# Weighting the quantile sums one step later in a four-layer graph kernel on Trainium2

## The chip, the core and the metric

The kernel runs on one core of one Trainium2 chip. The core has a matrix engine (TensorE, PE in the profile; its weight loads are shown apart as PEld), a vector engine (VectorE, DVE), a scalar engine (ScalarE, ACT), a general one (GpSimd, POOL) and one that here issues all transfers (SyncE, SP). TensorE writes its results to PSUM; VectorE and ScalarE read them there. The metric is device time in microseconds, as the median of several runs; lower is better.

## The reference, cut to what matters

There are 16 graphs of 1024 nodes with 64 channels, each with its own adjacency matrix, and four layers in turn. Every layer normalizes its input, applies a ReLU and adds its result to `x`. Layer 0 is where the change lies: it takes, for every node and channel, a weighted sum of three interpolated quantiles over the node's neighbours (the graph is thinned first), adds it to the node's own value and runs a two-layer perceptron.

```python
TAUS = [0.25, 0.5, 0.75]
QWEIGHTS = [0.25, 0.5, 0.25]
...
for tau, wt in zip(TAUS, QWEIGHTS):
    pos = jnp.clip(tau * (mf - 1.0), 0.0)
    lo = jnp.floor(pos).astype(jnp.int32)
    hi = jnp.ceil(pos).astype(jnp.int32)
    frac = (pos - lo.astype(x.dtype))[..., None]
    q = gather(lo) * (1.0 - frac) + gather(hi) * frac
    agg = agg + wt * q
...
adj_d = _dilate_adj(adj, mask)
agg = _weighted_nanquantile_agg(x, adj_d > 0)
out = (1.0 + EPS_GIN) * x + agg
h = jax.nn.relu(jnp.einsum('bnc,ch->bnh', out, W1) + b1)
y = jnp.einsum('bnh,ho->bno', h, W2) + b2
```

Layer 1 is a mean over neighbours, layer 2 attention with eight heads biased by the adjacency, layer 3 a graph convolution.

## The kernel before

**Two programs woven into one.** `picks` (L771) does layer 0's quantiles and `layers` (L1231) does the rest of every graph. Both are generators. The kernel's last loop draws a piece of `picks`, which gives back a price (0.42 for a step), and then pieces of `layers` until as much is spent; a block of 128 rows of attention for two heads costs 1.0. While the first graph is being picked, there is no layer work yet; after the last graph is picked, `layers` runs alone.

The framework traces the whole program in this way and then orders each engine's instructions at build time. What is traced earlier has the higher priority, but an instruction whose inputs or buffers are not there in the framework's own estimate is passed by others. `tc.issue_after(i)` adds that the instructions traced under it on the engine of `i` stay behind `i`. `adjoining` (L400) uses it to keep a series of matmuls together. On the chip each engine then runs its list in the given order.

**The steps of the picking.** `steps` (L777) lists graph `b` (16), channel group `g` of 8 channels (8), half `t` of 512 nodes (2) and quantile end `q` (6: lower and upper of three quantiles), 1536 in all. Six steps of the same `b`, `g`, `t` are called a group here; there are 256. A turn `n` of the main loop (L894) does, in this order:

- `next(coming)`: a piece of the tables for the next group. In the first two steps of a group the second such call of the turn also makes pair weights `e` (L697, L700) and `cw` (L702).
- `compare(n)` (L805): VectorE forms the mask `le` (L811) and the two masked words `wa` (L813) and `wb` (L815), each of 128x2048 half-precision numbers; TensorE sums them into `prep` and `val` (L826, L831); ScalarE copies these out as `wi` and `vs` (L837 to L840).
- `bits(n-1)` (L843): VectorE takes `bit` out of `wi`, TensorE builds `pz` from `bit` (L851) and `wi` (L852).
- `next(coming)` again.
- `value(n-2)` (L855): VectorE picks `vs` where `pz` tells it to (L859). When `q` is the last of six, TensorE sums the six into `agg` (L865, twelve instructions). VectorE multiplies `agg` by the interpolation coefficients `coef` into `w` (L874), TensorE sums `w` over the quantiles into the eight rows of `acc` (L876), ScalarE copies them back over the first eight rows of `w` (L877), and SP stores these in `z` (L878).
- after the last group of a graph, `leave` (L1036) runs the perceptron on `z`; then `next(behind)`, a piece of the ranking and thinning of the next graph, and the step ends.

**Buffers.** Tiles of one tag share its buffers. Tag a2 has four in SBUF, for `wi`, `bit`, `e`, `w` and a few rarer tiles. Tag pb has two in PSUM, for `agg` and `acc` and for nearly everything that TensorE makes in `layers`: the transposes `pcols` (L451), `ao` (L1183), `pp` (L1194), the projections `pk`, `pq` (L1131) and `pv` (L1143). Tag a4 has four, for `le`, `wa` and `wb`. A tile's buffer is free when its last reader is done; for `w` this is the store at L878.

Of the kernel before, what the change touches and what calls it, by code (L numbers as in the profile page):

```python
# [16 lines left out]
OP = mybir.AluOpType  # L17
# [21 lines left out]
def tile_preln_adj_stack(  # L39
# [30 lines left out]
    nc = tc.nc  # L70
    B, N, D = x.shape
# [12 lines left out]
    def a4(name, shape=(P, N), dt=F32):  # L84
        return sb.tile(list(shape), dt, tag="a4", bufs=4, name=name)
# [11 lines left out]
    def a2(name, shape=(P, 512), dt=F32):  # L97
        return sb.tile(list(shape), dt, tag="a2", bufs=4, name=name)

    def pa(name, shape=(P, 512), dt=F32):  # L100
        return ps.tile(list(shape), dt, tag="pa", bufs=2, name=name)
# [10 lines left out]
    def pb(name, shape=(P, 512), dt=F32):  # L112
        if alone and name != "pcols":
            return pa(name, shape, dt)
        return ps.tile(list(shape), dt, tag="pb", bufs=2, name=name)
# [124 lines left out]
    sel_c = const.tile([P, 8], F32, name="sel_c")  # L240
# [451 lines left out]
    def pair_weights(c0, rk):  # L692


        sh = [P, C, NBK, 2]
        e = a2("e", sh, HP)
        nc.vector.tensor_tensor(  # L697
            e, bc(k16[:, None, :, :], sh), bc(rk[:, :, None, c0 : c0 + 2], sh), OP.subtract
        )
        nc.vector.tensor_scalar(e, e, 0.0, 16.0, op0=OP.max, op1=OP.min)  # L700
        w = sb.tile(sh, I16, tag="cw", bufs=6, name="cw")
        act(w, e, AF.Copy, scale=1024.0)  # L702
        return w.bitcast(HP).rearrange("p c b s -> p c (b s)")
# [67 lines left out]
    def picks():  # L771

        steps = [  # L777
            (b, g, t, q) for b in range(B) for g in range(NG) for t in range(NH) for q in range(NQ)
        ]
        weights, tables, state, vs_of, els = {}, {}, {}, {}, {}  # L780

        def make(el, g, t):
            gen = group(el, g, t, weights)
            tables[el.b, g, t] = next(gen)
            if t == 0 and g < NG - 1:
                todo = [(el, g + 1, 0), (el, g + 1, 1)]
            elif t == 0:
                todo = []
            elif g < NG - 1:
                todo = [(el, g + 1, 2), (el, g + 1, 3)]  # L790
            else:
                todo = [(el.b + 1, 0, pp) for pp in range(4)] if el.b + 1 < B else []
            n = 0
            for _ in gen:
                if n % 2 == 1 and todo:
                    o, g2, pp = todo.pop(0)
                    o = els[o] if isinstance(o, int) else o
                    prepare(o, g2, pp)
                n += 1
                yield None  # L800

        def prepare(el, g, pp):
            weights.setdefault((el.b, g), {})[pp] = pair_weights(8 * g + 2 * pp, el.rk)

        def compare(n):  # L805
            b, g, t, q = steps[n]
            el = els[b]
            hs = slice(t * 512, (t + 1) * 512)
            cum, c1, c0 = tables[b, g, t]
            le = a4("le", (P, 4, 512), HP)  # L810
            nc.vector.tensor_tensor(le, cum, bc(el.krow[q][:, None, hs], [P, 4, 512]), OP.is_lt)  # L811
            wa = a4("wa", (P, 4, 512), HP)
            nc.vector.tensor_tensor(wa, le, c0, OP.mult)  # L813
            wb = a4("wb", (P, 4, 512), HP)
            nc.vector.tensor_tensor(wb, le, c1, OP.mult)  # L815
            prep, val = pa("prep"), pa("val")

            rounds = [
                (prep, [sel_w[:, 1, :]] * 4, [wb[:, pp, :] for pp in range(4)]),
                (prep, [sel_w[:, 0, :]] * 4, [wa[:, pp, :] for pp in range(4)]),  # L820
            ] + [
                (val, [el.tab[:, i, 4 * g + pp, :] for pp in range(4)], [le[:, pp, :] for pp in range(4)])
                for i in range(2)
            ]
            def made():
                yield nc.tensor.matmul(  # L826
                    prep, sel_q[:, q, :], el.kq[:, hs], start=True, stop=False, skip_group_check=True
                )
                for i, (dst, w, r) in enumerate(rounds):
                    for pp in range(4):  # L830
                        yield nc.tensor.matmul(  # L831
                            dst[32 * pp : 32 * pp + 32, :], w[pp], r[pp], start=i == 2, stop=i in (1, 3),
                            tile_position=(0, 32 * pp), skip_group_check=True,
                        )

            adjoining(made())
            wi = a2("wi")  # L837
            act(wi, prep, AF.Identity, bias=shifts[:, 5:6])
            vs = sb.tile([P, 512], F32, tag="v", bufs=8, name="vs")
            act(vs, val, AF.Copy, scale=1.0 / UP)  # L840
            state[n] = [wi, vs]

        def bits(n):  # L843
            wi, vs = state[n]
            bit = a2("bit", dt=I32)
            nc.vector.tensor_scalar(
                bit, wi.bitcast(I32), to30, 0x40000000, op0=OP.logical_shift_left, op1=OP.bitwise_and
            )
            pz = pa("pz")
            up = lambda x: x.bitcast(BF).rearrange("p (n two) -> p n two", two=2)[:, :, 1]  # L850
            nc.tensor.matmul(pz, nth, up(bit), start=True, stop=False)  # L851
            nc.tensor.matmul(pz, plus_k, up(wi), start=False, stop=True)  # L852
            state[n] = [pz, vs]

        def value(n):  # L855
            b, g, t, q = steps[n]
            el = els[b]
            pz, vs = state.pop(n)
            nc.vector.scalar_tensor_tensor(vs, pz, 97.0, vs, op0=OP.is_equal, op1=OP.mult)  # L859
            vs_of[q] = vs  # L860
            if q < NQ - 1:
                return
            agg = pb("agg")
            adjoining(
                nc.tensor.matmul(  # L865
                    agg[32 * (q_ % 4) : 32 * (q_ % 4) + 32, :], sel_t[:, q_ // 4, :], vs_of[q_],
                    start=q_ < 4, stop=q_ > 1, tile_position=(0, 32 * (q_ % 4)),
                    skip_group_check=True,
                )
                for q_ in range(NQ)  # L870
            )
            hs = slice(t * 512, (t + 1) * 512)
            w = a2("w")
            nc.vector.tensor_tensor(w, agg, el.coef[:, hs], OP.mult)  # L874
            acc = pb("acc", (8, 512))
            nc.tensor.matmul(acc, sel_c, w, start=True, stop=True)  # L876
            nc.scalar.copy(w[:8, :], acc)  # L877
            nc.sync.dma_start(el.z[t * D + 8 * g : t * D + 8 * g + 8, t, :], w[:8, :])  # L878

        els[0] = arrive(0)  # L880
        for r in background(0):
            yield 0.0
        for _ in els[0].stages:
            pass
        for pp in range(4):
            prepare(els[0], 0, pp)
        for _ in make(els[0], 0, 0):
            yield 0.05
        coming = behind = stages = iter(())


        STEPS = {12: 1, 11: 2, 10: 2, 9: 2, 8: 2, 7: 5, 6: 4, 5: 1, 4: 1, 3: 1, 2: 1, 1: 2}
        last, per = len(steps), NG * NH * NQ
        for n in range(last + 2):  # L894
            b, g, t, q = steps[min(n, last - 1)]
            to_go = per - n % per
            if n < last:
                if q == 0 and n + NQ < last:
                    coming = make(els[steps[n + NQ][0]], *steps[n + NQ][1:3])
                if to_go == per and b + 1 < B:  # L900
                    behind = background(b + 1)
                next(coming, None)
                compare(n)
                if to_go == 2 * NQ and b + 1 < B:


                    for _ in behind:
                        pass
                    els[b + 1] = arrive(b + 1)
                    stages = els[b + 1].stages  # L910
                for _ in range(STEPS.get(to_go, 0)):
                    next(stages, None)
            if 0 <= n - 1 < last:
                bits(n - 1)
            next(coming, None)
            if 0 <= n - 2:
                value(n - 2)
                if (n - 1) % per == 0:
                    leave(els.pop(steps[n - 2][0]))
                    for _ in stages:  # L920
                        pass
            next(behind, None)
            yield .42
# [356 lines left out]
```

## Time and profile before

| | us |
|---|---|
| median of 3 runs | 13374.41 (13370.68 to 13393.19) |
| the profiled execution's own time | 13383.01 |
| its span, first to last instruction | 13381.0 |
| granted TensorE clock, mean | 0.985 |
| `w` L874, 256 times: busy, idle of VectorE just before | 176.1, 132.5 |
| `agg` L865: PE busy | 592.5 |
| `acc` L876: PE busy | 263.1 |
| copy L877: ScalarE busy, idle just before | 144.9, 131.4 |

The profile is one execution. "Busy" is the time in which an instruction of the group ran; the idle time is that of the same engine directly ahead of such an instruction, with the instruction whose end released it. TensorE's matmuls are pipelined and their ends are modelled, so that its busy share is not a share of its peak. The idle time of one engine matters only where that engine, or one that waits for it, sets the pace.

### The profile page before, as it was taken

What the parts mean: (1) busy time and instruction counts of PE and PEld (TensorE: products, weight loads), DVE (VectorE), ACT (ScalarE), POOL (GpSimd) and SP (SyncE); (2) the same over time, 40 slices, a digit from 0 to 9 for tenths busy, and PEclk for the clock granted to TensorE, in tenths of its full rate; (3) what the DMA queues carried; (4) which work ended last, traced back from release to release, by engine and by line L of the source; (5) the groups of instructions that cost most, each with busy time, mean ns of one, the idle gap of its engine ahead of it and who ended that gap; (6) DMA issues with size and microseconds to landing.
All of it is one profiled execution on the core that took longest, in us unless ns stands there. A gap on an engine that the chain in (4) does not pass through costs nothing. (4 is left out here: it accounts for less than half of the span.)

```text
span 13381.0 us, 221273 instructions
## 1 busy us (share of the span) xinstructions
PE 12224.7 (91%) x86209; PEld 5569.6 (42%) x86209; DVE 11686.7 (87%) x21644; ACT 9477.1 (71%) x16250; POOL 25.6 (0%) x138
## 2 busy tenths in 40 slices
PE   1789999999999999999999999999999999999998
PEld 0224444444444444444444444444444444444445
DVE  8898989899898988989889898998989899887873
ACT  1557777677777776777767777777777777777766
POOL 0000000000000000000000000000000000000000
PEclk9999999999999999999999999999999999999999
DMA  3012121221212112121221212112121121301112
GB/s 100 30 39 66 51 86 49 62 73 53 82 52 88 50 57 75 50 88 52 65 66 56 82 53 70 63 56 81 53 83 48 60 80 52 94 30 60 33 50 74
DMA packets 503196, 841.35 MB, mean 63 GB/s; under 512 B 238720, under 2 KB 273664, under 8 KB 502144
## 3 DMA queue, kind: packets, MB, share of 16 engines
q1 hardware_dynamic: 502144, 827.20, 19.7%
q8 instruction: 675, 11.06, 0.3%
q14 instruction: 377, 3.09, 0.1%
HBM read 616.27 MB, written 206.57 MB: 61 GB/s over the span
## 5 line engine op out<-in xcount | busy, mean ns | idle before, releaser
L727 PE MATMUL px<-valid,cw 128*128 128x512 fp8e4 x8192 | 2072.7, 382 | 0.0
L813 DVE TENSOR_TENSOR wa<-le,c 128x2048 f16<-128x2048 f16 x1536 | 1870.2, 1218 | 152.4 <-PE prep L831 131.5
L811 DVE TENSOR_TENSOR le<-cum,krow 128x2048 f16<-128x2048 int16 x1536 | 1867.8, 1216 | 24.5 <-PE val L831 22.5
L815 DVE TENSOR_TENSOR wb<-le,c 128x2048 f16<-128x2048 f16 x1536 | 1868.8, 1217 | 15.5 <-PE prep L831 15.3
L398 ACT ACTIVATE c<-px,shifts 128x512 f16<-128x512 f32 x2048 | 1414.5, 694 | 347.1 <-PE px L748 172.5
L398 ACT ACTIVATE wi<-prep,shifts 128x512 f32<-128x512 f32 x1536 | 1061.8, 691 | 456.2 <-PE prep L831 364.1
L398 ACT ACTIVATE high<-px,shifts 128x512 f16<-128x512 f32 x1024 | 711.1, 694 | 910.5 <-PE px L727 908.0
L398 ACT ACTIVATE s<-s,nm 128x1024 f32<-128x1024 f32 x1024 | 1167.7, 1143 | 225.2 <-DVE nm L1173 217.4
L1183 PE MATMUL ao<-eT,v 128*64 128x128 f32 x16384 | 1272.4, 278 | 26.5 <-ACT eT L454 23.1
L727 PEld LDWEIGHTS <-cw 128*128 128x128 f16 x8192 | 800.4, 98 | 1147.0 <-issue 322.4
L831 PE MATMUL val<-le,tab 128*32 128x512 f16 x12288 | 1238.7, 386 | 30.1 <-DVE vs L859 22.8
L451 PE MATMUL pcols<-identf,s 128*128 128x128 f32 x8192 | 1175.3, 282 | 84.1 <-ACT eT L454 42.1
L1164 PE MATMUL sp<-kT,qT 64*128 64x512 f32 x4096 | 1166.3, 644 | 61.0 <-DVE nm L1173 59.6
L859 DVE SCALAR_TENSOR_TENSOR vs<-pz,vs 128x512 f32<-128x512 f32 x1536 | 1049.4, 683 | 142.6 <-PE pz L852 135.9
L451 PEld LDWEIGHTS pcols<-identf,s 128*128 128x128 f32 x8192 | 891.5, 141 | 631.0 <-ACT eT L454 252.8
L454 ACT COPY eT<-pcols 128x512 f32<-128x512 f32 x2048 | 1116.4, 597 | 51.9 <-PE pcols L451 47.7
L1183 PEld LDWEIGHTS ao<-eT,v 128*64 128x64 f32 x16384 | 962.6, 136 | 432.8 <-issue 208.9
L398 ACT ACTIVATE vs<-val 128x512 f32<-128x512 f32 x1536 | 923.8, 601 | 259.6 <-PE val L831 156.0
L831 PE MATMUL prep<-wb,sel_w 128*32 128x512 f16 x6144 | 783.1, 392 | 140.8 <-DVE wb L815 133.1
L831 PE MATMUL prep<-wa,sel_w 128*32 128x512 f16 x6144 | 852.4, 384 | 0.0
L1173 DVE CUSTOM_DVE_ANT_0 s<-sp,ad,nm 128x512 f32<-128x512 f32 x1024 | 730.7, 745 | 95.9 <-PE sp L1164 94.8
L1173 DVE CUSTOM_DVE_ANT_0 s<-sp,ad 128x512 f32<-128x512 f32 x1024 | 680.6, 684 | 105.4 <-PE sp L1164 80.1
(263 smaller groups left out, 19193.4 us busy)
## 6 DMA issues: line engine op xcount, KB each, us to landing
ad<-in_adj_dram SPq DMA_DIRECT2D x768, 512.0 KB
adjT_d<-aT SPq DMA_DIRECT2D x128, 512.0 KB
aT<-adjT_d SPq DMA_DIRECT2D x128, 512.0 KB
md<-sm SPq DMA_DIRECT2D x216, 256.0 KB
sb<-md SPq DMA_DIRECT2D x216, 256.0 KB
rem_d<-rem SPq DMA_DIRECT2D x128, 256.0 KB
left_d<-nb SPq DMA_DIRECT2D x128, 256.0 KB
lr<-left_d SPq DMA_DIRECT2D x256, 128.0 KB
```

The source lines that it names most:

```text
L398: nc.scalar.activation(out_, in_, func, **kw)
L451: nc.tensor.transpose(pt[:, c, :], ad[:, (4 * s + c) * P : (4 * s + c + 1) * P], identf)
L454: nc.scalar.copy(aT[:, 4 * s : 4 * s + 4, :], pt)
L727: yield nc.tensor.matmul(px[pp], w[:, j, :], valid[:, j, :], start=False, stop=j == C - 1, skip_group_check=True,)
L811: nc.vector.tensor_tensor(le, cum, bc(el.krow[q][:, None, hs], [P, 4, 512]), OP.is_lt)
L813: nc.vector.tensor_tensor(wa, le, c0, OP.mult)
L815: nc.vector.tensor_tensor(wb, le, c1, OP.mult)
L831: yield nc.tensor.matmul(dst[32 * pp : 32 * pp + 32, :], w[pp], r[pp], start=i == 2, stop=i in (1, 3), tile_position=(0, 32 * pp), skip_gr ...
L859: nc.vector.scalar_tensor_tensor(vs, pz, 97.0, vs, op0=OP.is_equal, op1=OP.mult)
L1164: nc.tensor.matmul(sps[e], qT[e * D : (e + 1) * D, i * P : (i + 1) * P], kT[e * D : (e + 1) * D, hs], start=True, stop=True,)
L1173: nc.vector.tensor_tensor_reduce(ss[e][:, hs], sps[e], ad[:, hs], -1.0, 3.0e38 if t == 0 else nms[e], op0=OP.add, op1=OP.min, accum_out=nm,)
L1183: nc.tensor.matmul(ao[e * D : (e + 1) * D, :], v[:, j, e * D : (e + 1) * D], eTs[e][:, j, :], start=j == 0, stop=j == C - 1, tile_position ...
```

## The change

The last part of `value`, from the multiply of `agg` to the store, becomes a function `weigh` that is put on a list `owing` and called later: in `compare` of the next turn, right after `wb`, with `tc.issue_after` on `wb`. After the last group of a graph it is called at once, before `leave`, with no such order. The multiply, the matmul, the copy and the store are the same; the tiles `w` and `acc` are asked for at the new place, and `agg`, whose matmuls stay where they were, is read there.

```diff
@@ -812,7 +812,9 @@
             wb = a4("wb", (P, 4, 512), HP)
-            nc.vector.tensor_tensor(wb, le, c1, OP.mult)
+            last = nc.vector.tensor_tensor(wb, le, c1, OP.mult)
+            while owing:
+                owing.pop()(last)
             prep, val = pa("prep"), pa("val")
@@ -869,13 +871,17 @@
-            hs = slice(t * 512, (t + 1) * 512)
-            w = a2("w")
-            nc.vector.tensor_tensor(w, agg, el.coef[:, hs], OP.mult)
-            acc = pb("acc", (8, 512))
-            nc.tensor.matmul(acc, sel_c, w, start=True, stop=True)
-            nc.scalar.copy(w[:8, :], acc)
-            nc.sync.dma_start(el.z[t * D + 8 * g : t * D + 8 * g + 8, t, :], w[:8, :])
+            def weigh(behind):
+                hs = slice(t * 512, (t + 1) * 512)
+                w = a2("w")
+                with tc.issue_after(behind.ins) if behind else ExitStack():
+                    nc.vector.tensor_tensor(w, agg, el.coef[:, hs], OP.mult)
+                acc = pb("acc", (8, 512))
+                nc.tensor.matmul(acc, sel_c, w, start=True, stop=True)
+                nc.scalar.copy(w[:8, :], acc)
+                nc.sync.dma_start(el.z[t * D + 8 * g : t * D + 8 * g + 8, t, :], w[:8, :])
+
+            owing.append(weigh)
@@ -916,6 +922,8 @@
                 if (n - 1) % per == 0:
+                    while owing:
+                        owing.pop()(None)
                     leave(els.pop(steps[n - 2][0]))
```

More of the change, by code (lines that the diff above doesn't have):

```diff
@@ L779, in picks @@
         ]
-        weights, tables, state, vs_of, els = {}, {}, {}, {}, {}
+        weights, tables, state, vs_of, els, owing = {}, {}, {}, {}, {}, []
         def make(el, g, t):
```

## The prediction

> **What bounds the kernel now.** I read the page's first part, then busy time by stage, then the groups of VectorE in the first stage, then its waits in the second, and last the order of time around one moved instruction. The page:
>
> ```profile
> span 13381.0 us, 221273 instructions
> ...
> PE 12224.7 (91%) x86209; PEld 5569.6 (42%) x86209; DVE 11686.7 (87%) x21644; ACT 9477.1 (71%) x16250; POOL 25.6 (0%) x138
> ...
> L813 DVE TENSOR_TENSOR wa<-le,c 128x2048 f16<-128x2048 f16 x1536 | 1870.2, 1218 | 152.4 <-PE prep L831 131.5
> ```
>
> TensorE and VectorE are both nearly full, and even the word `wa` waits for TensorE (131.5 us). The table of stages (from:to, length, then busy us of PE, PEld, DVE, ACT, POOL) parts the span where the first graph's picks start, where they end, and where the last graph's picks end:
>
> ```profile
> 370.00:1030.00 660.00, 543.30 (x2973) 164.59 (x2973) 611.25 (x845) 374.05 (x601) 0.00 (x0) 0.95 0.11 35
> 1030.00:12991.00 11961.00, 11280.37 (x80380) 5148.95 (x80378) 10622.33 (x19460) 8804.49 (x15125) 23.07 (x120) 0.99 0.20 63
> 12991.00:13381.00 390.00, 337.80 (x2561) 229.54 (x2560) 148.10 (x475) 231.25 (x421) 1.06 (x7) 0.87 0.26 83
> ```
>
> The first stage, where no layer of a graph runs yet, belongs to VectorE: 611.25 of 660 us, 93%, against 82% for PE. In the long middle stage PE has 94% and VectorE 89%. The tail has none of the moved work but its first instruction. Groups of VectorE in the first stage (busy us, mean ns | idle before, and what ended it):
>
> ```profile
> L811 DVE TENSOR_TENSOR le<-cum,krow 128x2048 f16<-128x2048 int16 x96 | 116.8, 1217 | 0.0
> L813 DVE TENSOR_TENSOR wa<-le,c 128x2048 f16<-128x2048 f16 x96 | 116.8, 1216 | 4.4 <-PE prep L831 4.3
> L815 DVE TENSOR_TENSOR wb<-le,c 128x2048 f16<-128x2048 f16 x96 | 116.8, 1216 | 2.6 <-PE prep L831 2.6
> ...
> L874 DVE TENSOR_TENSOR w<-agg,coef 128x512 f32<-128x512 f32 x16 | 11.1, 691 | 33.1 <-PE pz L851 31.5 <-PE agg L865 1.6
> ```
>
> Of 48.8 us that VectorE idles there, 33.1 lie ahead of the 16 weightings `w`, 2.1 us each. What ends them is `pz` L851, which is not what `w` reads. One of them in order of time (start, us, engine, line):
>
> ```profile
> 574.35 0.59 PE L865 MATMUL agg<-vs,sel_t 128*32 128x512 f32 x1
> ...
> 578.23 0.48 DVE L846 TENSOR_SCALAR bit<-wi,to 128x512 int32<-128x512 int32 x1
> ...
> 578.63 0.69 DVE L697 TENSOR_TENSOR e<-k,rk 128x1024 f16<-128x1024 f16 x1
> ...
> 579.39 0.68 ACT L398 ACTIVATE wi<-prep,shifts 128x512 f32<-128x512 f32 x1
> ...
> 580.91 0.39 PE L851 MATMUL pz<-bit,nth 128*128 128x512 bf16 x1
> ...
> 581.34 0.69 DVE L874 TENSOR_TENSOR w<-agg,coef 128x512 f32<-128x512 f32 x1 [2.02 <-PE pz L851]
> ```
>
> The sum `agg` is finished at 574.9; `w` starts 6.4 us later, right behind the matmul that reads `bit`. So it waits for a buffer: `wi`, `bit`, `e` and `w` share the four of tag a2, and the next `bit`, `e` and `wi` have just taken theirs. Middle stage, who waited for whom (us, times, longest):
>
> ```profile
> DVE xr L1196 <- PE pp L1194: 383.1, 188, 7.3
> DVE vs L859 <- PE pz L852: 131.8, 145, 5.7
> ...
> DVE w L874 <- PE agg L865: 64.0, 75, 5.6
> ...
> DVE w L874 <- PE pz L851: 23.8, 22, 3.9
> ```
>
> Here `w` has 87.8 us, in 97 waits, among far larger ones for PE.
>
> **What the Trainium skill says.** "PSUM — Partial Sum Buffer", section Engine vs sequencer instructions: VectorE's queue is strict first in, first out. The trace agrees: with `w` held 2.02 us nothing else of VectorE starts. "Perfetto Trace Analysis", section Optimization Strategy: the same gap recurring on the engine that should be saturated "can mean there isn't enough SBUF/PSUM for the next tile to be allocated". The gap of about 2 us in 13 of the first 16 groups, ended by a matmul that frees a buffer, is that case.
>
> **The change part by part.** No instruction is added or dropped: each group keeps one multiply (691 ns), two PE passes (592 ns each), one 8-row copy (566 ns mean) and one 16 KB store. For the last group of each graph all is done at once as before, so 240 of 256 groups move.
>
> *Where w goes.* I went through all groups in the trace, against the third `wb` after the last quantile's own (the next step's: a value is formed two steps after its words, in the turn before that `wb`): in 97 of 255 groups `w` starts before that `wb` ends, on average 4.0 us before; in 158 it is already behind it by 6.7 us on average, since there `agg` itself starts 11.6 us after its last input, held off by the two PSUM buffers of tag pb. The new order binds in the 97 only. Idle time before `w`: 63.8 us in the 97, 59.5 in the 158.
>
> *First stage.* 33.1 us of that idle time is here. At the new place, behind `le`, `wa`, `wb` (3 x 1.217 = 3.65 us, more than the usual wait), `pz` has read `bit` and `wi`, so two a2 buffers are free. In the sample `wb` could end near 582.1, where it now ends at 584.6, and `w` would start without a wait, `pz` having ended at 581.3. I leave out the last group (0.4 us, not moved) and 4 to 5 us for waits that come back as `wa` on `prep` or `bit` on a buffer. VectorE sets this stage and the layers can only start behind it: **-28 us**. Bounds: 0, if the wait moves on whole; -33.
>
> *Middle stage, groups that move.* 63.8 - 33.1 = 30.7 us. PE is the fuller engine; an earlier `wa` and `wb` let the next matmuls start earlier, but only where PE would have idled. I take half: **-15 us**. Bounds 0 and -31. The 59.5 us of the other groups I cost at nothing: they wait for `agg`, which doesn't move.
>
> *The agg buffer in PSUM.* It is held until `w` has read it, now a mean of 5.5 us (first matmul to end of `w`, 1413 us in all). The 97 groups hold it 4.0 us longer; in the first stage no layer wants it, leaving 82 x 4.0 = 330 us. From the start of the old `w` to the end of that `wb` (plus 0.7 us), two other tiles of the tag were live for 16.5 of 457 us, and none for 410: these are the very moments when the layers are not using it. All 16.5 us lost would be the most, I take **+12**. If that cover is gone, see the slower rival.
>
> *acc, copy and store.* They follow `w`. `acc` now asks for its buffer behind the layers' requests traced in between. PE's weight load for `acc` waited 63.2 us for `w` already and still will. The copy is ScalarE's, 71% busy. What sits behind the copy on ScalarE is the next `wi`; 0.57 us there is the same work in another place. SP's queue: the store is moved past at most a step's loads and stores (8.3 us: 11961/1440). SP stood 1100.8 us at this store for the copy in the middle stage, but 3762.1 at the adjacency loads for a free buffer, so these loads are not paced by the store. `z` is read only at the end of a graph. GpSimd's queue has none of it. No landing is recorded for the store, so the time that `w` holds its own a2 buffer isn't shown: I take no cost, bounds 0 to +20 (if `bit` waits a quarter of a microsecond in 80 groups).
>
> *Sum:* -28 - 15 + 12 = -31 on the span of 13381.0, 13350. The medians of the runs lie 6.6 us below that span, so the forecast is 13374.4 - 31 = **13343 us**.
>
> **The rivals.** *A, the forecast:* 13315 to 13360.
>
> *B, no measurable change, 13370.* The shortage of a2 buffers only changes hands: `w` keeps a buffer through copy and store while two `wi` and a `bit` want theirs, and `bit` stalls instead; PE absorbs the rest. For it: all four buffers stay, and the majority of groups don't move. Against: in the first two steps of each group only, `e` takes a fourth buffer, and the new place lies behind both.
>
> *C, slower, 13442.* One mechanism: `agg` holds one of two PSUM buffers through the next step in all 240 groups, the order of asking having changed for the late ones too, and the layers' transposes `pcols`, `ao` and `pp` go single file. Over the whole picking stage two other tiles of the tag are live 16.7% of the time. With a full step more (8.3 us) that is 240 x 8.3 x 0.167 = 333 us of lost overlap; with a third of it on the path +111, less the gains of 43, +68. It decides from about 3.2 us more per group (240 x 3.2 x 0.167 / 3 = 43), a mean hold of 8.7 us. For it: `agg` itself waits for this tag for 11.6 us in 158 groups, so the tag is short. Against: the 410 of 457 us.
>
> *D, much faster, 13250.* All 123 us of waiting ahead of `w` go and both engines use it. Against: 158 groups are behind already.
>
> *That the change does nothing it says* is the part of B in those 158 groups.
>
> **How the numbers follow.** A 0.42, D 0.06, B 0.24, C 0.28. About 0.2%, 27 us, is what a measurement of this kernel can tell from no change; A's point is 31 below, so its upper end touches B. Faster 0.48, same 0.24, slower 0.28. A and C being of both signs, A's own range stands above; the whole range goes down to 13285 (both gains in full, -64, and the rest of `w`'s waits in part) and up to 13435, nearly C's full price, since a moved request shifts the built order of every engine in ways that the trace of before can't show.
>
> **What would show it.** Right: idle ahead of `w` in the first stage falls from 33 us to under 5, the last pick of the first graph ends about 28 us earlier than 1025 us, `wb` keeps its 2.6 us, and `agg` is held 7 us or less on average. Wrong: `bit` or `wa` shows new waits of 20 us or more in that stage (B), or `agg`'s hold passes 8.7 us and waits for `pcols` and `ao` grow in the middle stage (C). A middle stage that grows by more than 28 us with neither of these would mean that the reordering of the rest decides, which no term of mine prices.

## The result and the profile after

| | before | changed |
|---|---|---|
| median of 12 runs each, us | 13380.35 (13370.45 to 13397.33) | 13355.42 (13342.54 to 13366.77) |
| ratio | | 0.998, 95% interval [0.9972, 0.9989] |
| span of the profiled execution, us | 13381.0 | 13353.8 |
| last pick of the first graph ends at, us | 1024.3 | 1023.1 |
| from there to the last pick of all, us | 11966.6 | 11940.8 |
| tail, us | 390.1 | 389.9 |

The change is 25 us faster; the forecast was 31. The lower rows say that the gain did not come from where the forecast had it: the first stage gave 1.2 us where 28 were forecast, and the middle stage 26 where 3 were.

Part of the difference goes with the granted TensorE clock, which is not the same in every run. Executions of the kernel before, from the later measurements, took a median of 13380.8 us at a mean clock of 0.986 (51 of them) and 13374.5 at 0.987 (14); those of the changed kernel took 13366.6 (3) and 13355.0 (5). At equal clock 14 to 20 of the 25 us are left. In the two profiles the middle stage ran at 0.9910 and 0.9920, so that, as an estimate, up to 12 of its 26 us can be the clock's.

The page of the changed kernel, and its table of stages (from:to, length, busy us of PE, PEld, DVE, ACT, POOL):

```profile
span 13353.8 us, 221219 instructions
...
PE 12203.7 (91%) x86209; PEld 5558.4 (42%) x86209; DVE 11682.2 (87%) x21644; ACT 9486.5 (71%) x16250; POOL 27.3 (0%) x138
```

```profile
370.00:1023.00 653.00, 544.87 (x2945) 163.92 (x2944) 607.20 (x836) 367.34 (x593) 0.00 (x0) 0.95 0.11 35
1023.00:12964.00 11941.00, 11261.13 (x80375) 5139.83 (x80375) 10620.69 (x19465) 8819.98 (x15131) 24.70 (x120) 0.99 0.20 63
12964.00:13354.00 390.00, 334.84 (x2594) 228.47 (x2594) 148.62 (x476) 231.32 (x422) 1.06 (x7) 0.89 0.26 84
```

The work is the same, and the shares of the whole run are as before. VectorE still has 93% of the first stage. Its waits there, in the changed kernel (us, times, longest):

```profile
DVE vs L861 <- PE pz L854: 21.9, 18, 3.4
DVE wa L813 <- PE prep L833: 5.3, 8, 1.8
DVE w L878 <- PE pz L853: 4.7, 4, 1.6
...
DVE bit L848 <- ACT cw L398: 2.9, 5, 0.8
```

The wait before `w` is nearly gone, as forecast: 31.1 us on `pz` have become 4.7. But `vs` (L859 before, L861 now), which waited 4.1 us, waits 21.9. All idle time of VectorE in this stage together went from 48.1 to 45.6 us. How that happens shows in one group. The changed kernel in order of time (start, us, engine, line), one step after a `w` at 664.56:

```profile
667.51 0.49 DVE L848 TENSOR_SCALAR bit<-wi,to 128x512 int32<-128x512 int32 x1 [0.53 <-ACT cw L398]
...
669.69 0.60 PE L880 MATMUL acc<-w,sel_c 128*8 128x512 f32 x1
...
670.98 1.02 PE L867 MATMUL agg<-vs,sel_t 128*32 128x512 f32 x2
...
671.93 0.40 PE L853 MATMUL pz<-bit,nth 128*128 128x512 bf16 x1
...
672.60 0.69 DVE L861 SCALAR_TENSOR_TENSOR vs<-pz,vs 128x512 f32<-128x512 f32 x1 [1.26 <-PE pz L854]
```

And the same group in the kernel before, where `w` is at 665.66:

```profile
666.83 1.03 PE L876 MATMUL acc<-w,sel_c 128*8 128x512 f32 x2
...
670.60 0.48 DVE L846 TENSOR_SCALAR bit<-wi,to 128x512 int32<-128x512 int32 x1
670.65 0.69 ACT L398 ACTIVATE high<-px,shifts 128x512 f16<-128x512 f32 x1 [1.62 <-PE px L727]
670.93 1.02 PE L865 MATMUL agg<-vs,sel_t 128*32 128x512 f32 x2
...
671.97 0.39 PE L851 MATMUL pz<-bit,nth 128*128 128x512 bf16 x1
...
673.27 0.68 DVE L859 SCALAR_TENSOR_TENSOR vs<-pz,vs 128x512 f32<-128x512 f32 x1
```

VectorE has `bit` ready three microseconds earlier now, at 668.0. TensorE takes it up at 671.93, as before at 671.97: it has the table matmuls, `val`, `acc` and `agg` ahead of it in its list. The two passes of `acc`, which ran early at 666.83, have moved into this full stretch. VectorE is early and waits.

In the middle stage the waits of VectorE that answer to those shown of before are these:

```profile
DVE xr L1204 <- PE pp L1202: 351.7, 187, 6.6
DVE vs L861 <- PE pz L854: 157.3, 158, 4.6
...
DVE w L878 <- PE agg L867: 67.7, 71, 4.3
```

`w`'s wait for a buffer (23.8 us on `pz`) is down to 3.9, `vs` has 25.5 us more, `xr` 31.4 less. The idle time of PE as shown hardly moves, 680.6 to 679.9 us over the stage. What moves is PE's weight load for `acc` (PEld: busy, mean ns | idle before it, what ended it), first before, then changed:

```profile
L876 PEld LDWEIGHTS acc<-w,sel_c 128*8 128x8 f32 x476 | 25.7, 87 | 143.6 <-DVE w L874 58.2 <-issue 31.4 <-DVE bit L846 16.5
```

```profile
L880 PEld LDWEIGHTS acc<-w,sel_c 128*8 128x8 f32 x478 | 25.5, 87 | 89.5 <-DVE w L878 33.1 <-issue 13.7 <-DVE bit L848 9.4
```

`acc` used to start 1.5 us after `w` on average and now starts 6.1 us after it, its place in the list now lying behind layer work that is traced before it. TensorE therefore meets `w` finished more often. From the start of the matmul before each `acc` to the start of `acc`, less the idle time of PE itself (gaps over 0.15 us), the trace of the middle stage adds up to 94.0 us before and 70.3 us now. That looked like 24 us saved on the fuller engine and made a new candidate for the gain, the *acc theory*. It does not hold: behind the experiments it is shown what this sum consists of.

### The profile page after: what moved, and what is told of

Same layout as the page of the kernel before. It is cut to its first block, busy times and chain, and to the rows that moved or that the text cites. A ratio compares the mean times of both kernels' runs of the same rounds, so it can differ in the third digit from the quotient of the medians.

```text
span 13353.8 us, 221219 instructions
## 1 busy us (share of the span) xinstructions
PE 12203.7 (91%) x86209; PEld 5558.4 (42%) x86209; DVE 11682.2 (87%) x21644; ACT 9486.5 (71%) x16250; POOL 27.3 (0%) x138
## 5 line engine op out<-in xcount | busy, mean ns | idle before, releaser
L861 DVE SCALAR_TENSOR_TENSOR vs<-pz,vs 128x512 f32<-128x512 f32 x1536 | 1054.4, 686 | 184.4 <-PE pz L854 179.2
```

## The experiments

Four theories went in. **P**, the prediction's own: VectorE sets the first stage, and `w`'s wait there is a loss. **R**: the wait is only relocated, since TensorE's order sets that stage. **Acc**: the middle stage gains because `acc` waits less for `w`; beside it the *buffer* theory, that `w`'s own wait for an a2 buffer is what is saved. **O**: order; any small change of the traced program gives every engine another list, and that alone moves the time by about as much.

**The first graph alone, and all but the first.**

```diff
-            owing.append(weigh)
+            owing.append(weigh) if b == 0 else weigh(None)
```

> Only the first graph's groups are weighted a step later; all others as before. Theory P (the prediction's own): the stage before the layers begin belongs to VectorE, so most of the 28 us must show here. Theory R (relocated): in that stage the wait before w merely moves to vs and bit, so the last pick of the first graph ends near 1023 us (1024.3 before, 1023.1 changed) and the whole is 0 to 5 us faster. Theory O (order by chance): the rest may go either way by 30 us, through nothing but another order of the built queues.

Measured: 13384.49 us against 13382.16 of before (ratio 1.0002 [0.9994, 1.0011]); the first stage ends at 1026.9 us. VectorE's waits in it:

```profile
DVE vs L861 <- PE pz L854: 23.1, 20, 3.4
DVE w L878 <- PE pz L853: 5.8, 4, 1.6
```

The wait has moved from `w` to `vs` here too, and the 28 us do not exist. P falls.

```diff
-            owing.append(weigh)
+            owing.append(weigh) if b > 0 else weigh(None)
```

> The complement: the first graph as before, the other fifteen weighted a step later. Theory R with the acc theory (TensorE waits less at acc, because acc is queued longer after w): 20 to 27 us faster, and the idle time of PE's weight load before acc in the middle stage falls from 145 us to about 90. Theory P: no more than 3 us. Theory O: anything within 30 us of before.

Measured: 13358.93 us, ratio 0.9984 [0.9977, 0.999], 23 us faster; weight load idle before `acc` in the middle stage 89.5 us. The whole gain is that of the other fifteen graphs. By graph it is not even: between the ends of their last picks, the second graph takes 780.3 us (790.9 before), the third 817.3 (846.6), the ninth 858.7 (825.9), the twelfth 811.3 (780.8). The changed kernel has nearly the same profile by graph, with 781.1, 816.1, 858.0 and 811.3. These swings of 30 us either way belong to the built order, not to chance at run time. P allowed 3 us here, and falls by this run too.

**acc alone a step later.** `w` is formed where it was; the deferred function holds `acc`, copy and store.

```diff
+            hs = slice(t * 512, (t + 1) * 512)
+            w = a2("w")
+            nc.vector.tensor_tensor(w, agg, el.coef[:, hs], OP.mult)
             def weigh(behind):
-                hs = slice(t * 512, (t + 1) * 512)
-                w = a2("w")
-                with tc.issue_after(behind.ins) if behind else ExitStack():
-                    nc.vector.tensor_tensor(w, agg, el.coef[:, hs], OP.mult)
                 acc = pb("acc", (8, 512))
```

> w is formed at the old place, only acc, its copy and its store come a step later, behind wb. Acc theory: the gain of the change is kept, 20 to 30 us faster, with PE's weight load idle before acc at 100 us or less in the middle stage, although VectorE's idle time before w stays near 130 us over the run. Buffer theory (the gain is w's wait for a buffer of tag a2): no gain, within 5 us of before. Slower rival C needs agg's long hold, which is gone here, so it expects this to be faster than the change.

Measured: 13373.23 us, ratio 0.9993 [0.9984, 1.0002]. The weight load's idle time fell to 92.3 us and the sum worked out above to 71.7, so the acc theory's means are there, but only 9 us of gain, and the interval reaches past no change. The idle time before `w` did not stay near 130 us over the run: it rose to 150.7. Nor is this kernel faster than the changed one, as rival C expected. PE's idle time in the middle stage is 702.5 us, 22 more than before.

**w later, acc at high priority.**

```diff
-                acc = pb("acc", (8, 512))
+                with tc.high_priority():
+                    acc = pb("acc", (8, 512))
```

(the matmul and the copy stand under it as well)

> w a step later as in the change, but acc and its copy at high priority, so that they follow w at once as before. Acc theory: PE's weight load again waits for w (over 130 us idle before acc in the middle stage) and the gain shrinks to under 8 us. Buffer theory: the gain of 20 to 25 us stays, since w's waits stay short.

Measured: 13350.33 us, ratio 0.9974 [0.9965, 0.9982]. This one does not decide: `acc` still starts 5.7 us after `w` on average, so it did not bring back what it was to bring back, and the weight load's idle time stayed at 90.1 us, where over 130 were expected.

**Orders that should make no difference.** The price of a step, 0.42, only says when layer work is woven in. Changing it by 0.0005 or 0.001 leaves every instruction as it is.

```diff
-            yield .42
+            yield .4195
```

(.4205 and .421 likewise, in both kernels)

> The kernel before with the price of a step at 0.4195 instead of 0.42: the same instructions, woven with the layers at slightly other points, so that the built order differs. Theory O (the gain of the change is the luck of an order): this moves the time by 15 us or more either way. Mechanism theories (acc or buffer): within 10 us of before, 13372 to 13392.

> The kernel before with the price of a step at 0.4205. Theory O: 15 us or more from before, either way and not as the price 0.4195 did. Mechanism theories: 13372 to 13392.

> The changed kernel with the price of a step at 0.4195. Mechanism theories: 25 us, give or take 10, below the kernel before with the same price. Theory O: no steady difference to that one; the sign may turn.

> The changed kernel with the price of a step at 0.4205. Mechanism theories: 25 us, give or take 10, below the kernel before with the same price. Theory O: no steady difference to that one.

> The kernel before with the price of a step at 0.421. Theory O: more than 15 us from before. Acc theory: PE's weight load idle before acc in the middle stage again 145 us, give or take 10.

> The changed kernel with the price of a step at 0.421. Acc theory with order as a second, independent term: weight load idle before acc 90 us, give or take 10; against the kernel before with this price about 24 us faster, give or take 55, so that the mean over the four prices lies near 24. Theory O alone: the mean over the four is not told from nothing.

Measured, with the ratios to the kernel before at 0.42 on the same chip (three sets of runs, in which the kernel before at 0.42 took 13380.35, 13383.21 and 13386.82 us):

| price of a step | before, us | changed, us | difference |
|---|---|---|---|
| 0.4195 | 13370.20, 0.9989 [0.9981, 0.9998] | 13386.12, 1.0002 [0.9994, 1.0011] | +15.9 |
| 0.42 | 13380.35 | 13355.42, 0.998 [0.9972, 0.9989] | -24.9 |
| 0.4205 | 13435.82, 1.004 [1.0025, 1.0054] | 13365.39, 0.9986 [0.9979, 0.9992] | -70.4 |
| 0.421 | 13398.25, 1.0009 [1.0, 1.0018] | 13408.88, 1.0018 [1.0009, 1.0026] | +10.6 |

The difference turns its sign twice. Its mean is -17 us and the four scatter by 40 (their standard deviation), so that the mean is known to about 20: by these times alone it is not told from nothing. The kernel before alone covers 66 us over four prices, the changed one 53. Each of these medians is known to about 0.1%; it is the order that differs. No theory's expectation holds throughout: against the same kernel at 0.42 on the same chip, the kernel before moved by -13, +53 and +11 us, where O asked for 15 and more, and the mechanism theories, in the first two, for 10 and less; and none of the three new pairs has the changed kernel 25 us faster, give or take 10.

What is steady under all four is the wait itself. The weight load for `acc` at price 0.4205, before and changed:

```profile
L876 PEld LDWEIGHTS acc<-w,sel_c 128*8 128x8 f32 x476 | 25.5, 87 | 151.0 <-DVE w L874 67.5 <-issue 25.7 <-DVE bit L846 18.0
```

```profile
L880 PEld LDWEIGHTS acc<-w,sel_c 128*8 128x8 f32 x478 | 24.9, 87 | 90.1 <-DVE w L878 36.7 <-DVE bit L848 12.6 <-issue 8.5
```

At the four prices the idle time before it is 145.9, 144.8, 152.2 and 151.8 us in the kernel before, and 85.8, 90.0, 91.8 and 92.5 in the changed one (all of the middle stage). The way from the matmul before to `acc`, worked out as above, is 91.9, 94.0, 95.1 and 97.9 us against 71.1, 70.3, 70.6 and 71.8.

**What the way to acc consists of.** It is as steady as the wait, but it is not a saving. From the start of one matmul to the start of the next passes, for the most part, the time of the first one, and the change has given `acc` other neighbours. The same group in the kernel before and in the changed one:

```profile
5998.49 1.13 PE L1164 MATMUL sp<-kT,qT 64*128 64x512 f32 x4
5999.55 1.02 PE L876 MATMUL acc<-w,sel_c 128*8 128x512 f32 x2
```

```profile
5949.01 1.13 PE L1172 MATMUL sp<-kT,qT 64*128 64x512 f32 x4
5950.06 0.49 PE L1202 MATMUL pp<-wproj,aoT 128*128 128x128 f32 x2
5950.48 1.02 PE L880 MATMUL acc<-w,sel_c 128*8 128x512 f32 x2
```

The four `sp` hold the next matmul off by 1.06 and 1.05 us; only which one comes next has changed. In the middle stage, counted in the traces at price 0.42:

| the matmul before `acc` | before: times, mean us to `acc` | changed | mean us to any other kind (`pp`: changed kernel) |
|---|---|---|---|
| `sp` | 86, 0.54 | 39, 0.54 | 0.53 |
| `px` | 107, 0.33 | 58, 0.31 | 0.29 |
| `pp` | none | 77, 0.21 | 0.15 |

With each neighbour's usual distance to another kind in place of that to `acc`, all of them add up to 92.6 us before and 67.5 in the changed kernel, so that next to nothing of the 24 us is `acc`'s own. What `acc` really saves is idle time of PE ahead of it: 16.4, 15.0, 18.6 and 17.1 us at the four prices before, 9.2, 10.7, 13.1 and 12.0 in the changed kernel, some 4 to 7 us.

**What the orders differ in.** `prep`, `val` and `agg` are matmuls in groups of 32 columns (128*32 in the profile). Call a run of them with no other kind between a *series*. The same matmuls stand in 3755 series of the middle stage in one built order and in 3983 in another. By graph, the changed kernel against the one before has 59 series fewer where the third graph is 31 us shorter, and 54 and 72 more where the ninth is 32 and the twelfth 31 us longer. Between the same code at two prices (six pairs of traces of 15 graphs each), a graph takes 0.43 us more for every series more, with a correlation of 0.86.

| price | series, before and changed | middle stage, us, before and changed | difference | left at 0.43 us a series |
|---|---|---|---|---|
| 0.4195 | 3768, 3855 | 11963.9, 11975.7 | +11.8 | -26 |
| 0.42 | 3755, 3755 | 11966.6, 11940.8 | -25.8 | -26 |
| 0.4205 | 3890, 3846 | 12027.4, 11955.4 | -72.1 | -53 |
| 0.421 | 3776, 3983 | 11993.3, 12018.7 | +25.4 | -64 |

In the traces at 0.4195 and 0.4205 about a thousand records of `pz` are missing, nearly all of its second pass, so that their counts can be off by a little. With the number of series taken out, the changed kernel is shorter in all four orders, by 42 us on average with a standard error of about 11; the clock can account for some 6 of these. These are estimates from one profile each, made after the runs; no kernel was built that keeps its series whole, so that the price of a series is a correlation and not shown by experiment. It does not name the cause of what is left either. For one kernel that rest is known to about 20 us only: -22 for all but the first graph, -32 for `acc` at high priority, -9 for `acc` alone a step later.

**w in other buffers, nothing moved.** Tag v has eight buffers for `vs`; six of them have been given back when `agg` is done.

```diff
-            w = a2("w")
+            w = sb.tile([P, 512], F32, tag="v", bufs=8, name="w")
```

> The kernel before, with w put into the eight buffers of tag v (six of which agg has just given back) instead of the four of tag a2; nothing is moved. Theory P (VectorE sets the first stage and w's wait for a buffer is its loss): w's 33 us of idle in that stage go and its last pick ends near 995 to 1000 us. Theory R (TensorE's order sets it): the waits come back ahead of vs, and the stage ends within 5 us of 1024. The whole time says nothing here, within 40 us of before by theory O.

Measured: 13329.25 us, ratio 0.996 [0.9946, 0.9975], the fastest of all kernels here. The first stage ends at 1015.4 us, between the two theories. VectorE's waits there:

```profile
DVE vs L859 <- PE pz L852: 12.9, 19, 1.5
DVE w L874 <- PE agg L865: 7.4, 8, 1.6
```

The 31.1 us of `w` on `pz` are gone, so it was a buffer that `w` waited for. `vs` and `w` take back 14.6 us (`vs` 4.1 to 12.9, `w` on `agg` 1.6 to 7.4), and some 9 us of the stage are won: outside the 1022.3 to 1026.1 us at which it ends in the kernels that leave the first graph's `w` and its buffer alone, and the 1019.4 to 1026.9 of those that move that `w` in the a2 buffers. That is a third of what P wanted. The rest lies in the middle stage (11930.8 us against 11966.6 in the profiles) and can't be told from a lucky order with one such kernel, though 13329 lies 41 us below the fastest of four orders of the kernel before; it has 17 series fewer, which at 0.43 us are 7 of its 36 us there.

The same with the change:

> The changed kernel with w in the buffers of tag v. If the waits of the first stage come back through w's hold of a buffer of tag a2 up to its store, vs loses most of its 22 us of idle there, bit its 3 and w its 5, and the stage ends near 1000 us. If TensorE's order sets the pace (theory R), vs keeps over 15 us and the stage ends within 5 us of 1023.

Measured: 13349.97 us, ratio 0.9974 [0.9965, 0.9984]; the first stage ends at 1024.1 us.

```profile
DVE vs L861 <- PE pz L854: 29.2, 25, 3.5
```

With the a2 buffers out of the way `bit` and `w` do not wait any more in this stage, and `vs` waits longer than ever, for TensorE. R holds for the changed place: the same buffers end the stage 9 us earlier with `w` and `acc` where they were.

## Why the prediction was right in its number and wrong in its sum

The time, 13355, lies in the range and on the side that was forecast, 12 us from the point. By its own bound of 0.2% (27 us) it is just inside what counts as no change, though the measured interval leaves out 1. That the total came so close is luck: 28 us that did not come were made up by 23 more in the middle stage than forecast, and at three other prices the same change gave +16, -70 and +11 us. The steps fared as follows.

- *Where w goes:* right. 251 of 255 weightings now start behind their `wb`; the idle time before `w` fell from 132.5 to 86.3 us over the run and from 33.1 to 5.1 us in the first stage (under 5 was forecast, just missed). That it was a buffer is shown by the run that gave `w` other buffers.
- *First stage, -28:* the step that failed. "VectorE sets this stage" was read from its 93%. Removing its largest wait gave 1.2 us (at the other three prices -0.6 to 4.6), because PE's list has `pz` behind a stretch of other matmuls that is full; the stretch is shown for one group, the waits of `vs` for the whole stage. The prediction saw that `w` was released by `pz`; it did not ask when `pz` would be there for the next reader, `vs`. The lower bound that it kept, "0, if the wait moves on whole", is nearly what came, and the place named for it was wrong: `vs` on `pz`, not `wa` or `bit`.
- *Middle stage, -15 +12:* -26 in this order. The buffer wait that it counted went, 23.8 to 3.9 us, and VectorE's idle time fell by 19 us of 1339. Whether that is where the gain comes from is not shown: in two other orders the stage grew, where it also has 87 and 207 series more. An estimate with the series taken out leaves a gain of 26 to 64 us in all four.
- *acc:* "PE's weight load waited 63.2 us already and still will" was wrong as it stands: the idle time before the load fell by 55 us. Its price, nothing, was nearly right: PE itself lost 4 us less ahead of `acc`. The prediction named what puts `acc` later, its request behind the layers' ones (argued, not tried by itself).
- *agg in PSUM:* held 6.6 us on average, 5.5 before; under the 7 that was forecast and far from the 8.7 at which rival C decides. C's cause didn't arise. Two of four pairs are slower all the same, by a reordering that the prediction said it could not price.
- *SP's queue and the copy:* nothing in the traces speaks against costing them at nothing; that was not tried by itself.

What stays open is the cause of what the changed kernel saves beside the number of its series: the buffer that `w` no longer waits for is the candidate that is left, argued and not shown.

## What to carry to other kernels

A wait that ends at another engine's instruction is worth removing only if that engine could have delivered the next thing earlier too: look up in its list what stands before the next delivery. And where a scheduler weaves two programs, measure how far an indifferent change moves the time (here 66 us over four orders, 0.5%) before a gain of 0.2% is called a gain, and count what the orders differ in. A sum of times between the starts of neighbouring instructions holds the work of the first of each pair: compare it only between equal neighbours. If a short tile waits in a crowded pool of buffers, try a pool that has just been emptied before moving the instruction.

## What was not expected of the hardware

When the `prep` matmuls of the four column groups stand together, the four start within 0.01 us and the next four 0.23 us after them. Where the list alternates single ones with the full-width `px`, each of either kind starts 0.32 us after the one before. Both are from the changed kernel, at a granted clock of 1.0:

```profile
564.91 0.40 PE L833 MATMUL prep<-wb,sel_w 128*32 128x512 f16 x4
565.14 0.39 PE L833 MATMUL prep<-wa,sel_w 128*32 128x512 f16 x4
...
658.57 0.38 PE L727 MATMUL px<-valid,cw 128*128 128x512 fp8e4 x1
658.88 0.39 PE L833 MATMUL prep<-wb,sel_w 128*32 128x512 f16 x1
659.20 0.39 PE L727 MATMUL px<-valid,cw 128*128 128x512 fp8e4 x1
```

This goes on to 663.37, so that eight of each take 5.1 us. Together they would take about 2.2, as an estimate: two times 0.23, and eight at the 0.22 us of an unbroken run of `px` (1.89 us for eight, the last one 0.38 long). That is 2.9 us for seven series more, 0.41 us each, close to the 0.43 us that a series more goes with in the middle stage. Both kernels have such stretches in the first stage, right ahead of the waits that this study followed.
